# Moving the self products of 24 row blocks into the next stage's first slots, and building one-hots on ScalarE in the last two steps of a graph network

## The chip, the cores and the metric

The kernel runs on one core of a Trainium2 chip. The metric is the device time of one execution in microseconds (us); lower is better. The engines named below are PE (TensorE: matrix products), DVE (VectorE), ACT (ScalarE), POOL (GpSimd, which issues the indirect DMAs that gather rows) and SP (SyncE, which issues the plain DMAs). Everything is float32.

## The reference

There are 10,000 nodes with 512 features and 160,000 edges sorted by destination; every edge has one of four types. Two layers follow each other, each on `h = relu(layernorm(x))` and each with a residual.

```python
# layer 0
h_all = einsum('nd,rdf->nrf', x, rel_W) + rel_b        # one product per node and edge type
agg   = segment_sum(h_all[src, edge_type], dst) / max(deg, 1)
x1    = layer_norm(x + x @ self_W + self_b + agg)      # x here is the layer's h
out   = layer_norm(x1 + gelu(x1 @ W1 + b1) @ W2 + b2)
# layer 1, twice with its own weights
h_neigh = segment_sum(h[src], dst) / max(deg, 1)
h = relu(h @ W_self + h_neigh @ W_neigh + b)
```

## The kernel before

The 10,000 rows are cut into 78 blocks of 128 rows and a last one of 16 rows (block number `full` = 78). The program has three parts, one after the other, because each gathers rows from a DRAM table that the part before must have written completely.

**The relation stage.** It goes over 39 sets of two blocks (and the short block first). For each set it normalizes the rows, transposes them on PE into `hT`, forms the four relation products by a scheme with seven half products instead of eight (`times`, line 717), and writes them to the table `hall_d`. Within it `residual` (lines 648 to 655) forms the self product of each block: four matmuls of `hT` with `wself` (to whose diagonal 1 was added, so that it also carries the residual `x`), then a DVE addition of `bself`; `stored` (lines 663 to 666) writes the sum to `xs_d`. A generator `step` puts the preparation of the edge lists (which rows each block gathers) between these products; its last pieces run in the first half of the last twelve sets. Here the framework's scheduler may reorder instructions.

**The feed-forward stage.** From here on (`aligned`, line 752) the order is as written. One slot per block, the short one first. In a slot the kernel gathers the rows of the next block (`gather`, line 765), builds its one-hot matrices (`hots`, line 782), sums the shared rows with one-hot matmuls (`sums`, line 790) and adds 11 rows per lane with DVE additions (`add`, line 804). A full block takes 11 such gathers (`row`), 5 (`orow`) for `sums`, and now and then one into `tail`; each brings 128 rows of 2 KB. The gathered tiles `rows` come from a ring of 28 buffers. After the additions the slot normalizes its block, and PE runs a piece of the feed-forward products of the group of four blocks before (`queue`, `products`): half of the up products or two down products. The queue is filled when the first block of the next group has gone by, so the first slots have almost nothing in it. The tiles `po`, `h1` and `xr` of the profile belong to this stage; `po` has two PSUM buffers.

**The last two steps.** Each goes over the 79 blocks and gathers from `h1_d` or `h2_d` in the same way. A slot has the self product (`wss`, line 1134), the neighbour product of the block before (`finish`, line 1100), the transposition of the next block, then `begin` for the next block, which gathers and runs `sums`. In all three gathering stages `hots` is one DVE comparison of 128x896 elements per block:

```python
nc.vector.tensor_tensor(hot[:, :n], lane[:, None, :].to_broadcast([P, n, P]),
                        loc[:, b, :n].unsqueeze(2).to_broadcast([P, n, P]),
                        op=OP.is_equal)
```

Of the kernel before, what the change touches and what calls it, by code (L numbers as in the profile page):

```python
# [8 lines left out]
F32 = mybir.dt.float32  # L9
# [3 lines left out]
AF = mybir.ActivationFunctionType  # L13
# [3 lines left out]
P = 128  # L17
# [4 lines left out]
def kernel(  # L22
# [77 lines left out]
    dram = ctx.enter_context(tc.tile_pool(name="dram", bufs=1, space=DRAM))  # L100

    hall_d = dram.tile([N + P, R * D], F32, name="hall_d")
    xs_d = dram.tile([N, D], F32, name="xs_d")
# [484 lines left out]
    with ExitStack() as s:  # L588
# [58 lines left out]

        def residual(rows, r, c, pm):
            xg, _, hg, _ = rows
            h = hg[:r, c, :]  # L650
            nc.vector.tensor_tensor(xg[:r, c, :], xg[:r, c, :], ln2b[:r], op=OP.add)
            for k in range(KC):
                nc.tensor.matmul(pm[:r], rows[3][:, c, k, :r], wself[:, k, :], start=(k == 0),  # L653
                                 stop=(k == KC - 1))
            nc.vector.tensor_tensor(h, pm[:r], bself[:r], op=OP.add)
# [7 lines left out]
        def stored(g, rows):  # L663
            b0, nb, r = g
            nc.sync.dma_start(rows_of(xs_d, g), rows[2][:r, :nb])
            nc.sync.dma_start(rows_of(xr_d, g), rows[0][:r, :nb])
# [7 lines left out]
        if N % P:  # L674
            r = sets[0][2]
            residual(rows, r, 0, psM.tile([P, D], F32, name="pm"))
            for j in sorted(range(R), key=lambda j: (j % RH, j)):
                pm = psM.tile([P, D], F32, name="pm")
                for k in range(KC):
                    nc.tensor.matmul(pm[:r], rows[3][:, 0, k, :r], wrel[j][:, k, :],  # L680
                                     start=(k == 0), stop=(k == KC - 1))
                ha = ap_.tile([P, D], F32, name="u2")
                nc.vector.tensor_tensor(ha[:r], pm[:r], bias(j)[:r], op=OP.add)
                message(full, j, ha, r)
            stored(sets[0], rows)
# [14 lines left out]
        for i, g in enumerate(sets):  # L700
# [7 lines left out]

            def times(pm, a, w, start, stop):
                for k in range(KH):  # L710
                    nc.tensor.matmul(pm, a[:, k, :], w[:, k, :], start=(start and k == 0),
                                     stop=(stop and k == KH - 1))

            def times(a, w):
# [6 lines left out]
            for j in range(RH):  # L721
# [12 lines left out]
                if j == 0 and later:  # L734
                    rows_next = opened(later)
                residual(rows, P, j, psM.tile([P, D], F32, name="pm"))
                if later:
# [14 lines left out]
    def aligned(ctxa):  # L752
# [28 lines left out]

        def hots(b):
            n = OT + NL if b < full else OT_LAST
            hot = gat.tile([P, OT + NL, P], F32, name="hot", bufs=2)
            nc.vector.tensor_tensor(hot[:, :n], lane[:, None, :].to_broadcast([P, n, P]),  # L785
                                    loc[:, b, :n].unsqueeze(2).to_broadcast([P, n, P]),
                                    op=OP.is_equal)
            return hot

        def sums(b, others, hot):  # L790

            r, n = height(b), len(others)
            pa = psA.tile([P, D], F32, name="pa")
            order = list(range(n)) if b == full else list(range(OT, n))[::-1] + list(range(OT))
            for t in order:
                nc.tensor.matmul(pa[:r], hot[:, t, :r], others[t], start=(t == order[0]),  # L796
                                 stop=(t == order[-1]))
            return pa

        def begin(b, hot, table):  # L800
            others, mine = gather(b, table)
            return sums(b, others, hot), mine

# [7 lines left out]
        with ExitStack() as s:  # L811
# [34 lines left out]
            def column(row, name):  # L846
# [3 lines left out]
                return t  # L850

            for b in blocks[:2]:
                load(b)
            ln1w = wide(wp, ln1_w, D, "ln1w")
            lnb2 = wide(wp, ln1_b, D, "lnb2")
# [146 lines left out]
            def products(work, turned):  # L1002
# [10 lines left out]
                if not work:  # L1013
                    yield
                    if turned:
                        turned()
                fed = [g for g in got if g]

            i = 0
            grp = None  # L1020
            for bs in plan:
                for b in bs:
# [5 lines left out]
                    if i + 1 < len(blocks):  # L1028
                        hot = hots(blocks[i + 1])
                    got = second()  # L1030
                    pa, mine = held
# [32 lines left out]
        for step, (h_d, ws, wn, bs) in enumerate(((h1_d, ws1, wn1, bs1), (h2_d, ws2, wn2, bs2))):  # L1064
            with ExitStack() as s:
# [52 lines left out]
                before = None  # L1118
                held = begin(blocks[0], hots(blocks[0]), h_d)
                for i, b in enumerate(blocks):  # L1120
# [4 lines left out]
                    if i + 1 < len(blocks):  # L1125
                        hot = hots(blocks[i + 1])
                    pa, mine = held
# [10 lines left out]
                    if i + 1 < len(blocks):  # L1138
                        turn(blocks[i + 1])
                        held = begin(blocks[i + 1], hot, h_d)  # L1140
                    mT = ip.tile([P, KC, P], F32, name="mTb")
# [4 lines left out]
    def general():  # L1146
# [141 lines left out]
        with ExitStack() as s:  # L1288
# [8 lines left out]
            ln1w = wide(vp, ln1_w, D, "ln1w")  # L1297
            ln1b = wide(vp, ln1_b, D, "ln1b")
            for g in groups:
                b0, nb, r = g  # L1300
# [152 lines left out]
```

## Time and profile before

| | |
|---|---|
| time, median of 3 runs | 6363.47 us (6357.54 to 6369.66) |
| the profiled execution: its own time, its span | 6372.26 us, 6370.5 us |
| mean granted PE clock | 0.935 |
| busy: PE, DVE, ACT, POOL | 5484.2, 3734.8, 1356.8, 3824.4 us |
| relation stage, to the last DVE addition | 0 to 1318 us |
| first gather of the feed-forward stage | 1321.38 us |
| last gather of it | 2975.57 us |
| gathers of the first of the two steps, first and last | 3076.55 and 4708.84 us |
| gathers of the second step, first and last | 4726.08 and 6350.45 us |

The share of busy time of an engine is a mean over stages with different limits. The table of stretches therefore says more than the totals: in the relation stage POOL has little to do, and in the other stages it issues one gather after the other. A row of the groups gives busy time, then the mean duration of one instruction in ns, then the idle time of the engine before these instructions and what ended it. One matmul of 128x512 in float32 is two records.

### The profile page before, as it was taken

What the parts mean: (1) busy time and instruction counts of PE and PEld (TensorE: products, weight loads), DVE (VectorE), ACT (ScalarE), POOL (GpSimd) and SP (SyncE); (2) the same over time, 40 slices, a digit from 0 to 9 for tenths busy, and PEclk for the clock granted to TensorE, in tenths of its full rate; (3) what the DMA queues carried; (4) which work ended last, traced back from release to release, by engine and by line L of the source; (5) the groups of instructions that cost most, each with busy time, mean ns of one, the idle gap of its engine ahead of it and who ended that gap; (6) DMA issues with size and microseconds to landing.
All of it is one profiled execution on the core that took longest, in us unless ns stands there. A gap on an engine that the chain in (4) does not pass through costs nothing.

```text
span 6370.5 us, 50895 instructions
## 1 busy us (share of the span) xinstructions
PE 5484.2 (86%) x13939; PEld 2410.3 (38%) x13939; DVE 3734.8 (59%) x7361; ACT 1356.8 (21%) x2391; POOL 3824.4 (60%) x3927
## 2 busy tenths in 40 slices
PE   9999999969999999999777777777777777777777
PEld 4544444434444444444333333333333333333333
DVE  8768888556777777776344444444444444444444
ACT  1025665013333333333111111111110000000000
POOL 0001110057777777775577777777767777777776
PEclk9999999989999999999888889889889898888998
DMA  4233333267878777886677777777777777777776
GB/s 165 108 116 124 119 119 121 109 211 243 254 246 255 249 253 254 253 256 188 192 232 233 232 231 228 226 233 233 225 237 246 244 241 243 246 246 246 247 237 204
DMA packets 491734, 1360.90 MB, mean 214 GB/s; under 512 B 76606, under 2 KB 76606, under 8 KB 491310
## 3 DMA queue, kind: packets, MB, share of 16 engines
q0 software_dynamic: 308768, 1008.91, 52.1%
q1 hardware_dynamic: 182142, 347.60, 15.3%
q8 instruction: 112, 1.84, 0.1%
q14 instruction: 184, 1.51, 0.1%
q10 hardware_dynamic: 528, 1.05, 0.0%
HBM read 1150.25 MB, written 207.01 MB: 213 GB/s over the span
## 4 chain that ended last, share of the span: by engine, by line
DMA 34%; PE 8%; issue 4%; POOL 4%; DVE 1%; POOLq 0%; ACT 0%; DVEq 0%; SPq 0%; ACTq 0%
DMA rows<-h_d,row 21%; DMA rows<-h_d,orow 12%; PE pa L796 4%; POOL rows L769 4%; PE po L1134 2%; PE po L1100 2%; DMA tail<-h_d,srow 1%; DVE pa L808 1%; PE pT L167 1%; DVE ob L1110 0%; DMA wns<-in_L_gnn_W_neigh_dram 0%; DMA hb<-h_d 0%; POOLq L769 0%; DVE hot L785 0%; POOL tail L769 0%
## 5 line engine op out<-in xcount | busy, mean ns | idle before, releaser
L808 DVE TENSOR_TENSOR pa<-pa,rows 128x512 f32<-128x512 f32 x2574 | 1798.7, 699 | 1999.0 <-DMA rows<-h_d,row 887.4
L796 PE MATMUL pa<-rows,hot 128*128 128x512 f32 (+1 forms) x2358 | 1381.6, 723 | 675.7 <-DMA rows<-h_d,orow 617.6
L769 POOL DMA_INDIRECT rows<-h_d,row x1716 | 1638.1, 955 | 524.1 <-issue 206.2
L796 PEld LDWEIGHTS pa<-rows,hot 128*128 128x128 f32 (+1 forms) x2358 | 488.8, 225 | 1555.5 <-DMA rows<-h_d,orow 1105.5
L769 POOL DMA_INDIRECT rows<-hall_d,row x858 | 868.6, 1012 | 261.4 <-issue 101.8
L769 POOL DMA_INDIRECT rows<-h_d,orow x786 | 795.0, 1012 | 355.1 <-issue 195.1
L769 POOL DMA_INDIRECT rows<-hall_d,orow x393 | 371.9, 946 | 379.9 <-SPq L1449 258.6
L903 PE MATMUL po<-w2s,hid 128*128 128x512 f32 (+1 forms) x1264 | 561.8, 598 | 26.3 <-DVE rest L959 26.2
L796 PE MATMUL pa<-tail,hot 128*128 128x512 f32 x936 | 476.5, 627 | 114.9 <-DMA tail<-h_d,srow 93.8
L1100 PE MATMUL po<-wns,mTb 128*128 128x512 f32 (+1 forms) x1264 | 572.0, 595 | 1.5 <-ACT mTb L168 1.5
L1134 PE MATMUL po<-wss,hTb 128*128 128x512 f32 (+1 forms) x1264 | 573.2, 596 | 0.0
L892 PE MATMUL ph<-x1T,w1s 128*128 128x512 f32 (+2 forms) x1344 | 558.5, 568 | 4.8 <-ACT hid L894 4.8
L1130 ACT ACTIVATE mb<-pa,rdeg 128x512 f32<-128x512 f32 (+1 forms) x158 | 108.5, 687 | 1822.0 <-DVE pa L808 1813.1
L503 POOL DMA_INDIRECT win<-rec_d,at x79 | 75.5, 956 | 578.8 <-PE pe L528 500.1
L903 PEld LDWEIGHTS po<-w2s,hid 128*128 128x128 f32 (+1 forms) x1264 | 236.3, 190 | 321.3 <-issue 279.6
L1100 PEld LDWEIGHTS po<-wns,mTb 128*128 128x128 f32 (+1 forms) x1264 | 239.7, 190 | 307.3 <-issue 305.2
L892 PEld LDWEIGHTS ph<-x1T,w1s 128*128 128x128 f32 x1344 | 249.3, 191 | 281.9 <-issue 271.4
L168 ACT COPY mTb<-pT 128x512 f32<-128x512 f32 (+1 forms) x158 | 91.7, 580 | 1108.6 <-PE pT L167 1108.6
L1134 PEld LDWEIGHTS po<-wss,hTb 128*128 128x128 f32 (+1 forms) x1264 | 229.5, 192 | 232.2 <-issue 232.1
L717 PE MATMUL pm<-wrel,hT 128*128 128x512 f32 x624 | 296.6, 598 | 0.0
L717 PE MATMUL pm<-wrel,s 128*128 128x512 f32 x624 | 293.3, 592 | 0.0
L653 PE MATMUL pm<-wself,hT 128*128 128x512 f32 (+1 forms) x632 | 287.0, 597 | 1.0 <-DVE wself L670 1.0
(272 smaller groups left out, 5249.5 us busy)
## 6 DMA issues: line engine op xcount, KB each, us to landing
hall_d<-p SPq DMA_DIRECT2D x156, 256.0 KB, 2.5
hall_d<-u SPq DMA_DIRECT2D x156, 256.0 KB, 2.4
hb<-h_d SPq DMA_DIRECT2D x38, 1024.0 KB, 7.3
rows<-h_d,row POOLq DMA_INDIRECT x1716, 3.7
xg<-in_x_dram SPq DMA_DIRECT2D x39, 512.0 KB, 3.7
xr_d<-xg SPq DMA_DIRECT2D x39, 512.0 KB, 3.0
xs_d<-hg SPq DMA_DIRECT2D x39, 512.0 KB, 2.8
xs<-xs_d SPq DMA_DIRECT2D x39, 512.0 KB, 7.9
```

Of the source, the lines that this page charges most:

```text
L168: nc.scalar.copy(dest, p[:, :, :r])
L503: nc.gpsimd.indirect_dma_start(out=win[:, c, :], out_offset=None, in_=rec_d, in_offset=bass.IndirectOffsetOnAxis(ap=at[:, c:c + 1], axis=0))
L653: nc.tensor.matmul(pm[:r], rows[3][:, c, k, :r], wself[:, k, :], start=(k == 0), stop=(k == KC - 1))
L717: nc.tensor.matmul(pm, a[:, k, :], w[:, k, :], start=(k == 0), stop=(k == KH - 1))
L769: nc.gpsimd.indirect_dma_start(out=t[:n], out_offset=None, in_=table, in_offset=bass.IndirectOffsetOnAxis(ap=idx, axis=0))
L796: nc.tensor.matmul(pa[:r], hot[:, t, :r], others[t], start=(t == order[0]), stop=(t == order[-1]))
L808: nc.vector.tensor_tensor(pa[:r], pa[:r], t[:r], op=OP.add)
L892: nc.tensor.matmul(ph[:, :n], w1s[:, k, f * P:(f + 1) * P], self.xT[:, k, :n], start=(k == 0), stop=(k == KC - 1))
L903: nc.tensor.matmul(po[:r], self.hid[:, f, c * r:(c + 1) * r], w2s[:, f, :], start=(f == 0), stop=(f == FC - 1))
L1100: nc.tensor.matmul(po[:r], mT[:, k, :r], wns[:, k, :], start=False, stop=(k == KC - 1))
L1130: nc.scalar.activation(m[:r], pa[:r], AF.Copy, scale=rdeg[:r, b:b + 1])
L1134: nc.tensor.matmul(po[:r], hT[:, k, :r], wss[:, k, :], start=(k == 0), stop=False)
```

## The change

The self products of the last 24 blocks (54 to 77, twelve sets) are no longer formed in the relation stage. Their transposed rows `hT` go to a new DRAM tensor `hT_d`, one DMA of 256 KB per block, and `xs_d` of these sets is not written there. The feed-forward stage loads `self_W` and `self_b` again, into buffers of the tiles `xr` and `h1`, fetches 3 of the 24 blocks ahead of its first slot and 4, 4, 3, 3, 3, 4 in the slots 0 to 5 (into tiles of the ring `rows`), forms their products at the end of the slot's piece of PE work and ahead of `begin`, and stores them to `xs_d`, where their own slots load them much later. In the last two steps `hots` is built by ACT: seven activations |loc - lane| of 128x128, and one relu(1 - that) over all 128x896. There `sums` is preceded by three products of the identity matrix with a slice of `wss` into the same PSUM tile, which the first product of `sums` overwrites.

The program's other branch (for edge lists that do not fit, not taken here) gets the products of the 24 blocks too; that part is left out.

```diff
+    LATE_SETS = 12
+    late = list(range(full - 2 * LATE_SETS, full))
+    hT_d = dram.tile([len(late) * P, D], F32, name="hT_d")
...
-        def residual(rows, r, c, pm):
-            xg, _, hg, _ = rows
+        def residual(rows, r, c, b):
+            xg, _, hg, hT = rows
             h = hg[:r, c, :]
             nc.vector.tensor_tensor(xg[:r, c, :], xg[:r, c, :], ln2b[:r], op=OP.add)
+            if b in late:
+                i = late.index(b)
+                nc.sync.dma_start(hT_d[i * P:(i + 1) * P, :], hT[:, c].rearrange("p k n -> p (k n)"))
+                return
+            pm = psM.tile([P, D], F32, name="pm")
             for k in range(KC):
                 nc.tensor.matmul(pm[:r], rows[3][:, c, k, :r], wself[:, k, :], start=(k == 0),
                                  stop=(k == KC - 1))
...
         def stored(g, rows):
             b0, nb, r = g
-            nc.sync.dma_start(rows_of(xs_d, g), rows[2][:r, :nb])
+            if b0 not in late:
+                nc.sync.dma_start(rows_of(xs_d, g), rows[2][:r, :nb])
             nc.sync.dma_start(rows_of(xr_d, g), rows[0][:r, :nb])
...
-        def hots(b):
+        def hots(b, scalar=False):
             n = OT + NL if b < full else OT_LAST
             hot = gat.tile([P, OT + NL, P], F32, name="hot", bufs=2)
+            if scalar:
+                for t in range(n):
+                    nc.scalar.activation(hot[:, t, :], lane, AF.Abs, bias=loc[:, b, t:t + 1],
+                                         scale=-1.0)
+                nc.scalar.activation(hot[:, :n], hot[:, :n], AF.Relu, bias=ones[:, :1], scale=-1.0)
+                return hot
...
+        def keep_busy(p, w, n):
+
+            for _ in range(n):
+                nc.tensor.matmul(p, ident, w, start=True, stop=True)
+
-        def sums(b, others, hot):
+        def sums(b, others, hot, idle=None):
 
             r, n = height(b), len(others)
             pa = psA.tile([P, D], F32, name="pa")
+            if idle:
+                keep_busy(pa, *idle)
...
+            FIRST_LATE, LATE = 3, (4, 4, 3, 3, 3, 4)
+            assert FIRST_LATE + sum(LATE) == len(late)
+            ws = [gp.tile([P, 2, D], F32, name="xr", bufs=3) for _ in range(2)]
+            selfb = gp.tile([P, 2, D], F32, name="h1", bufs=2)[:, 0, :]
+            waiting, arrived = list(late), {}
+
+            def fetch(n):
+
+                for b in waiting[:n]:
+                    i = late.index(b)
+                    t = gat.tile([P, D], F32, name="rows", bufs=RING)
+                    nc.sync.dma_start(t, hT_d[i * P:(i + 1) * P, :])
+                    arrived[b] = t
+                del waiting[:n]
+
+            def residuals():
+
+                for b, t in arrived.items():
+                    po = psO.tile([P, D], F32, name="po")
+                    for k in range(KC):
+                        nc.tensor.matmul(po, t[:, k * P:(k + 1) * P], ws[k // 2][:, k % 2, :],
+                                         start=(k == 0), stop=(k == KC - 1))
+                    nc.vector.tensor_tensor(t, po, selfb, op=OP.add)
+                    nc.sync.dma_start(xs_d[b * P:(b + 1) * P, :], t)
+                arrived.clear()
+
+            for i, w in enumerate(ws):
+                nc.sync.dma_start(w, self_w[i * 2 * P:(i + 1) * 2 * P, :].rearrange(
+                    "(k p) n -> p k n", p=P))
+            nc.sync.dma_start(selfb, bass.AP(tensor=self_b.tensor, offset=self_b.offset,
+                                          ap=[[0, P], [1, D]]))
+            fetch(FIRST_LATE)
             for b in blocks[:2]:
                 load(b)
+            for k in range(KC):
+                at = ws[k // 2][:, k % 2, k * P:(k + 1) * P]
+                nc.vector.tensor_tensor(at, at, ident, op=OP.add)
+            residuals()
             ln1w = wide(wp, ln1_w, D, "ln1w")
             lnb2 = wide(wp, ln1_b, D, "lnb2")
...
+                residuals()
                 fed = [g for g in got if g]
...
                         hot = hots(blocks[i + 1])
+                    if i < len(LATE):
+                        fetch(LATE[i])
                     got = second()
...
-                held = begin(blocks[0], hots(blocks[0]), h_d)
+                held = begin(blocks[0], hots(blocks[0], True), h_d)
...
-                        hot = hots(blocks[i + 1])
+                        hot = hots(blocks[i + 1], True)
...
-                        held = begin(blocks[i + 1], hot, h_d)
+                        held = begin(blocks[i + 1], hot, h_d, (wss[:, 0, :], 3))
```

## The prediction

> **What bounds the kernel now.** I read the table of stretches first, one stretch from each stage (columns: stretch, length, then busy us and instructions of PE, PE's weight loads, DVE, ACT, POOL; then PE clock, DMA share, GB/s).
>
> ```profile
> 960.00:1120.00 160.00, 160.00 (x527) 74.92 (x526) 133.69 (x558) 82.03 (x168) 12.41 (x13) 1.00 0.34 118
> 1280.00:1440.00 160.00, 105.93 (x273) 46.10 (x272) 82.69 (x134) 21.45 (x42) 88.72 (x91) 0.78 0.67 218
> 2080.00:2240.00 160.00, 154.85 (x380) 69.21 (x379) 119.47 (x199) 51.90 (x85) 122.23 (x125) 0.99 0.81 256
> 5120.00:5280.00 160.00, 122.70 (x290) 50.91 (x288) 77.29 (x109) 13.39 (x23) 121.93 (x126) 0.89 0.78 245
> ```
>
> The relation stage (first line) is PE without a gap. In the gathering stages POOL looks only 76% busy, but each gather carries 0.30 us around its 0.945 us, so 125 gathers need 125 x 1.25 = 156 of 160 us. POOL is the bound in both; in the feed-forward stage PE (155 us) is just behind it. Next, POOL's groups in the last two steps and the largest DVE and ACT entries there:
>
> ```profile
> L769 POOL DMA_INDIRECT rows<-h_d,row x1716 | 1638.1, 955 | 524.1 <-issue 206.2 <-DMA rows<-h_d,row 193.1 <-DMA rows<-h_d,orow 58.2
> L769 POOL DMA_INDIRECT rows<-h_d,orow x786 | 795.0, 1012 | 355.1 <-issue 195.1 <-DMA rows<-h_d,row 73.4 <-DMA rows<-h_d,orow 28.9
> L785 DVE TENSOR_TENSOR hot<-lane,loc 128x896 f32<-128x896 f32 x156 | 169.2, 1085 | 34.1 <-PE pa L796 34.1
> L1130 ACT ACTIVATE mb<-pa,rdeg 128x512 f32<-128x512 f32 x156 | 107.2, 687 | 1813.1 <-DVE pa L808 1813.1
> ```
>
> POOL's idle time is 0.30 us times its count: it never waits for a ring buffer. But its means, 955 and 1012 ns, are above 945. The timeline of a slot shows why:
>
> ```profile
> 3250.47 0.95 POOL L769 DMA_INDIRECT rows<-h_d,orow  x1 [0.30 <-DMA rows<-h_d,row]
> 3251.55 1.08 DVE L785 TENSOR_TENSOR hot<-lane,loc 128x896 f32<-128x896 f32 x1
> 3251.72 0.62 ACT L1111 ACTIVATE ob<-ob 128x512 f32<-128x512 f32 x1
> 3251.72 1.73 POOL L769 DMA_INDIRECT rows<-h_d,orow  x1 [0.30 <-DVE ob L1110]
> 3253.75 0.95 POOL L769 DMA_INDIRECT rows<-h_d,orow  x1 [0.30 <-issue]
> ```
>
> A gather that starts under the one-hot comparison ends 0.82 us after it: POOL stands still until DVE is done. Last, the joint of the first two stages: the timeline of its start, then PE's waits from 1318 to 1446.
>
> ```profile
> 1322.83 0.37 SPq L857 DMA_DIRECT2D h<-in_L_gnn_b_dram  x1
> 1331.01 0.69 DVE L859 TENSOR_TENSOR lnb<-lnb,h 128x512 f32<-128x512 f32 x1 [12.90 <-DMA ln1bc<-in_L_gnn_ln_b_dram]
> ...
> PE pa L796 <- DMA rows<-hall_d,orow: 34.1, 4, 11.7
> PE pa L796 <- DVE hot L785: 15.0, 1, 15.0
> PE pa L796 <- DMA tail<-hall_d,srow: 4.7, 1, 4.7
> ```
>
> PE has 54 us of gaps there, which the moved products are to fill.
>
> **Part 1, the relation stage.** In the timeline a self product starts at 1231.35 and PE's next work at 1234.78: 3.43 us. 24 of them are 82 us of a stage that is PE alone. Their DVE additions (L655, 0.69 us) go too. In the first half of the twelve sets the list preparation is there: sets are 32.8 us apart, and DVE is busy for 133.69/160 of that, 27.4 us. After the change PE needs 32.8 - 6.9 = 25.9 us a set and DVE 27.4 - 1.4 = 26.0. They now wait on each other; I take 1 us a set for six sets. The stores swap 12 DMAs of 512 KB for 24 of 256 KB on SP, at 0.37 us of issue each beside a set of 25 us: nothing, as PE waits for no store. **Gain 76 us** (bounds: 65, where DVE loses 3 us a set, and 82).
>
> **Part 2, the first slots.** They take the 24 products again; what counts is how far POOL is held back, as it never idles later.
>
> *Start.* SP now issues first the two halves of `self_W`, the bias and three row blocks, six DMAs of some 0.4 us and 2 MB. A 1 MB weight load took 6.2 us to land in the steps (`wss`), so the products start near 1329. PE is cold (0.84 us a record at 1332, later 0.43): 24 records take about 12.5 us, to 1341. Behind them stand three stores on SP, and behind these all of the parameter loads that DVE's L859 and then `hot` and the first `sums` wait for. The trace shows no SP wait for a store. The Trainium skill's page "DMA: Bandwidth & Descriptors" (section "Anatomy of one DMA — SWDGE (gpsimd) path") says that a semaphore wait happens on the issuing sequencer before dispatch, so later DMAs of that queue wait too. By the rows alone (issues of 0.4 us) the start would slip 3 us plus the PE work, 10 us; by the rule the bias load goes out at 1344, lands 7.9 us later as it does now, and the first `sums` starts at 1353 instead of 1332.4. I take the rule: 20 us.
>
> *Slots.* A slot with n moved products: two run at once on PE, but `po` has two buffers, and the third waits for a DVE addition queued behind this slot's 11 row additions and its normalization. In the trace that normalization runs from 1357.6 to 1362.4, so about 5.5 us after the row additions. Then products 3 and 4 end 9.7 and 13.1 us after the row additions, `sums` takes 6.1 us (14 records of 0.43) and the next 11 additions 8 us: 27 us a slot with four, 24 with three, against POOL's 21. From the start at 1353 the row additions of blocks 0 to 5 end near 1386, 1413, 1437, 1461, 1485, 1512; before they ended at 1357.6, 1375.5, 1395.9, 1416.2, 1437.9, 1459.0. DVE and PE are then 53 us late. POOL may run ahead by the ring of 28, less the tiles of moved rows, which come free only when their store has landed (some 3 us): counted tile by tile, block 6's gathers end near 1508 instead of 1476, 32 us late. From then on POOL runs at its pace of before and can't make up; PE, 20.3 us of work a block (154.85 us for 7.63 blocks) against POOL's 20.96, closes 0.65 us a block and has made up the 21 us between them within the 72 blocks left. The drain of 100 us to 3076 stays. **Loss 33 us** (bounds 12, if only PE's excess of 82 - 54 = 28 us counted and half were absorbed, and 70, if no slot overlapped).
>
> **Part 3, one-hots on ACT.** With no stretched gathers, 2552 gathers save their excess: 1638.1 + 795.0 + 47.3 = 2480.4 us busy, less 2552 x 0.945 = 2411.6, is **69 us gained** (0.44 us a block), all on POOL's path. What ACT does instead: a 128x512 activation from SBUF took 0.80 us (L945) and a 128x1 one 0.295, so 0.42 for 128 elements and 1.19 for 896: 7 x 0.42 + 1.19 = 4.1 us a block, 644 us against DVE's 169. This is covered: ACT waits 1813 us for DVE in front of L1130, 11.6 us a block, and the one-hots stand just ahead of it in ACT's queue. Without that cover it would cost 4.1 us x 156. ACT might stop POOL as DVE does: the gather above ended as DVE's end dictates although ACT worked from SBUF (L1111) beside it, so I take none.
>
> **Part 4, identity products.** 3 x 2 records x 0.43 = 2.6 us a block. PE has 122.70/7.7 = 16.0 us a block at clock 0.89 and POOL now sets 20.4, so they fill idle time; at 18.6 us nothing waits. Do they gain? The rows show PE waiting 4.6 us a block for `orow` and `tail` rows (617.6 + 93.8 us in 156 blocks). The skill's page "TensorE: Matmul & The Clock Gate" (section "What's actually happening") says that one idle window of some 3.4 us brings half rate back, which speaks against them: they run ahead of that wait, not through it. By the rule the clock stays near 0.89; if they kept it at 1.0, PE's own work without them would be 30 x 0.43 + 0.9 = 13.8 us. Both lie under 20.4, so 0 us either way.
>
> **Sum.** -76 + 33 - 69 = -112 us from the profiled execution's 6372.3, to 6260. Its run was 8.8 us above the median of 6363.5; less 112 that is **6252 us**.
>
> **Rivals.** *The first slots eat all of part 1.* For it: PE's gaps (54 us) are smaller than the 82 us moved, the ring and two `po` buffers tie the slots together. Against: POOL may run a block ahead. Loss 76, only part 3 left: 6363 - 69 = 6294. *The slots fill smoothly.* The parameter loads aren't held up and the third product isn't either; loss 10: 6363 - 76 + 10 - 69 = 6228. *The steps give little,* because another transfer or the latency (3.7 us to land) limits the gathers once POOL doesn't stall; against it, the DMA share of 0.78. Half of part 3: 6286. *Slower: PE becomes the bound of the last two steps.* The identity products lengthen each slot; if the clock falls, so does everything. At full clock PE's work is 36 records of 0.43 plus transposes of 0.9: 16.4 us a block. Parts 1 and 2 bring 43 us, so the steps must lose 56 us, 0.36 a block on 20.8: that is PE above 21.2 us, a mean clock under 0.77. At 0.70 a block takes 23.4 us, +2.6 x 156 = 406: about 6720. The row shows 0.89 and more work should not lower it. That ACT's one-hots never reach the path as a gain because POOL isn't stopped by DVE at all is excluded by the timeline above.
>
> **How the numbers follow.** Likeliest course 0.60 (6230 to 6275 from the bounds of the parts); first slots eat it all 0.14; smooth slots 0.12; half of part 3 0.09; slower 0.03; about no change, where part 1 and most of part 3 both come to nothing, 0.02. The range 6212 to 6300 takes in the first three and most of the fourth. A measurement tells 0.2% (13 us) from no change: faster 0.95, same 0.02, slower 0.03.
>
> **What would show it.** Right: L653 has 24 blocks fewer and the relation stage ends near 1242; in the next stage the first `sums` waits behind L912 and comes 31 to 32 us after the stage's first gather (11 before); POOL shows real waits in the first seven slots, some 30 us, and none later; in the steps both groups of gathers have means near 945 ns and each step's gathers span about 1594 us (1632 and 1624 before). Wrong: gather means that stay near 1000 (ACT stops POOL too), POOL waiting for PE or ACT in the steps, gaps in the relation stage's PE, or POOL waits of 70 us in the first slots.

## The result and the profile after

The changed kernel takes 6287.03 us (median of 4 runs, 6282.08 to 6287.47); in the same comparison the kernel before takes 6364.49. The ratio is 0.9877, 95% interval 0.986 to 0.9894: 77 us less. The forecast was 6252, with a range of 6212 to 6300: the direction and the range were right, the gain was overestimated by 35 us. The likeliest course, 6230 to 6275, was missed.

The profiled executions show where. Each program is cut at its gathers (from the timelines of POOL); a stretch runs from the start of one gather to that of another:

| stretch, us | before | after | difference | predicted |
|---|---|---|---|---|
| start to first gather from `hall_d` | 1321.4 | 1240.1 | -81.3 | -76 |
| first to last gather from `hall_d` (feed-forward stage) | 1654.2 | 1717.2 | +63.0 | +33 |
| last of these to the first gather of step 1 | 101.0 | 103.4 | +2.4 | 0 |
| gathers of step 1 | 1632.3 | 1593.5 | -38.8 | -69 for both |
| joint | 17.2 | 15.7 | -1.5 | 0 |
| gathers of step 2 | 1624.4 | 1594.8 | -29.6 | |
| rest | 20.1 | 20.0 | 0 | 0 |

The sum is -85.7, the difference of the two spans (6370.5 and 6284.8). Three of the four sizes were right; the first slots of the feed-forward stage cost almost twice what was set down for them. Of the 35 us, 26 lie in this table: 30 too little for those slots, less 5 that the relation stage gave beyond its forecast. The other 9 lie in the base: the profiled execution of the kernel before took 8 us more than its median (6372.26 and 6364.49), that of the changed kernel did not (6286.86 and 6287.03). In which stage the kernel before had these 8 us, one trace can't tell.

The table of stretches of the changed kernel, one from each stage as before (the second is the start of the feed-forward stage):

```profile
960.00:1120.00 160.00, 159.03 (x525) 74.86 (x524) 143.59 (x578) 82.16 (x167) 10.46 (x11) 1.00 0.44 150
1200.00:1360.00 160.00, 116.05 (x273) 51.47 (x272) 59.20 (x98) 11.26 (x22) 56.17 (x60) 0.83 0.64 211
2400.00:2560.00 160.00, 156.42 (x382) 69.61 (x382) 119.22 (x199) 51.91 (x85) 122.27 (x124) 0.99 0.81 254
5120.00:5280.00 160.00, 139.82 (x342) 60.99 (x341) 69.07 (x101) 35.97 (x80) 121.00 (x129) 0.93 0.80 249
```

In the first line DVE is 143.6 of 160 us and PE 159: the relation stage, with 24 products fewer, is still PE's. The last line has POOL at 121.00 us, almost as before (121.93), but with 129 gathers instead of 126: each is shorter. The groups of the last two steps say the same (the gathers, then the one-hots on ACT):

```profile
L773 POOL DMA_INDIRECT rows<-h_d,row x1716 | 1622.2, 945 | 523.6 <-issue 240.3 <-DMA rows<-h_d,row 156.3 <-DMA rows<-h_d,orow 67.0
L773 POOL DMA_INDIRECT rows<-h_d,orow x786 | 743.1, 945 | 356.0 <-issue 106.0 <-DMA h_d<-h 102.5 <-DMA rows<-h_d,row 53.9
L791 ACT ACTIVATE hot<-lane,loc 128x128 f32<-128x128 f32 x1098 | 337.7, 391 | 0.0
L793 ACT ACTIVATE hot<-hot,ones 128x896 f32<-128x896 f32 (+1 forms) x158 | 163.7, 1036 | 5.1
L1186 ACT ACTIVATE mb<-pa,rdeg 128x512 f32<-128x512 f32 (+1 forms) x158 | 108.5, 687 | 1226.9 <-DVE pa L825 1222.9 <-PE pa L813 4.0
```

Both means are 945 ns (955 and 1012 before). ACT's one-hots cost (337.7 + 163.7)/158 = 3.2 us a block, below the 4.1 estimated, and ACT still waits 1223 us for DVE ahead of L1186. PE waited for these one-hots twice, 3.7 us in all, so they are as good as covered.

The joint of the first two stages is where the missing 30 us are. SP's timeline there (start, duration of the issue):

```profile
1255.44 7.19 SPq L892 DMA_DIRECT2D xs_d<-rows  x3
...
1263.68 0.51 SPq L910 DMA_DIRECT2D h<-in_L_gnn_b_dram  x1
...
1266.35 1.56 SPq L914 DMA_DIRECT2D w1s<-in_L_gnn_W_dram  x1
1267.95 5.17 SPq L915 DMA_DIRECT2D b1s<-in_L_gnn_b_dram  x1
1273.16 5.93 SPq L917 DMA_DIRECT2D w2s<-in_L_gnn_W_dram  x1
1279.14 4.43 SPq L143 DMA_DIRECT2D ln2w<-in_L_gnn_ln_w_dram  x1
1283.61 1.89 SPq L880 DMA_DIRECT2D rows<-hT_d  x4
```

and PE's timeline of the same time:

```profile
1248.15 13.40 PE L889 MATMUL po<-xr,rows 128*128 128x512 f32 x24 [12.21 <-DMA rows<-hT_d]
1273.95 4.65 PE L813 MATMUL pa<-rows,hot 128*16 128x512 f32 x6 [12.40 <-DVE hot L795]
1291.91 15.45 PE L889 MATMUL po<-xr,rows 128*128 128x512 f32 x32 [13.31 <-DMA rows<-hT_d]
```

PE's waits from 1240 to 1450 (us in total, times, longest):

```profile
PE po L889 <- DMA rows<-hT_d: 26.4, 4, 13.3
PE po L889 <- DVE rows L891: 20.3, 5, 7.6
PE pa L813 <- DVE hot L795: 12.4, 1, 12.4
```

Before, PE had 54 us of gaps here, and the moved products were to fill them. It still has 59. A balance closes on that: 82 us of products moved, less 54 of gaps that are gone, plus 59 new ones, is 87; the row additions of block 5 end 221.1 us after the first gather instead of 137.6, which is 83.4 late. So the question for the experiments was which of the new waits are needed. e1 to e8 are single runs.

### The profile page after: what moved, and what is told of

Its sections match the earlier page's. It is cut to its first block, busy times and chain, and to the rows that moved or that the text cites. A ratio compares the mean times of both kernels' runs of the same rounds, so it can differ in the third digit from the quotient of the medians.

```text
span 6284.8 us, 53719 instructions
## 1 busy us (share of the span) xinstructions
PE 5753.7 (92%) x14875; PEld 2566.8 (41%) x14875; DVE 3573.7 (57%) x7207; ACT 1842.8 (29%) x3647; POOL 3756.4 (60%) x3927
## 4 chain that ended last, share of the span: by engine, by line
DMA 29%; PE 14%; issue 4%; POOL 3%; DVE 1%; POOLq 0%; ACT 0%; DVEq 0%; ACTq 0%; SPq 0%
DMA rows<-h_d,row 16%; DMA rows<-h_d,orow 12%; PE pa L813 5%; PE po L1190 4%; POOL rows L773 3%; PE po L1156 3%; PE pa L803 1%; PE pT L170 1%; DVE pa L825 1%; DMA tail<-h_d,srow 0%; DMA hb<-h_d 0%; DVE po L1162 0%; POOLq L773 0%; POOL tail L773 0%; DVE ob L1166 0%
## 5 line engine op out<-in xcount | busy, mean ns | idle before, releaser
L813 PE MATMUL pa<-rows,hot 128*128 128x512 f32 (+1 forms) x2358 | 1242.5, 660 | 373.4 <-DMA rows<-h_d,orow 350.0
L773 POOL DMA_INDIRECT rows<-h_d,orow x786 | 743.1, 945 | 356.0 <-issue 106.0
L813 PEld LDWEIGHTS pa<-rows,hot 128*128 128x128 f32 (+1 forms) x2358 | 449.1, 204 | 1124.5 <-DMA rows<-h_d,orow 723.1
L1190 PE MATMUL po<-wss,hTb 128*128 128x512 f32 (+1 forms) x1264 | 598.5, 618 | 0.0
L773 POOL DMA_INDIRECT rows<-hall_d,orow x393 | 376.6, 958 | 351.2 <-SPq L1520 203.2
L813 PE MATMUL pa<-tail,hot 128*128 128x512 f32 x936 | 447.2, 598 | 24.4 <-DMA tail<-h_d,srow 12.7
L1186 ACT ACTIVATE mb<-pa,rdeg 128x512 f32<-128x512 f32 (+1 forms) x158 | 108.5, 687 | 1226.9 <-DVE pa L825 1222.9
L803 PE MATMUL pa<-wss,ident 128*128 128x512 f32 x936 | 427.5, 593 | 0.0
L791 ACT ACTIVATE hot<-lane,loc 128x128 f32<-128x128 f32 x1098 | 337.7, 391 | 0.0
```

Source lines behind the costliest of these rows:

```text
L773: nc.gpsimd.indirect_dma_start(out=t[:n], out_offset=None, in_=table, in_offset=bass.IndirectOffsetOnAxis(ap=idx, axis=0))
L791: nc.scalar.activation(hot[:, t, :], lane, AF.Abs, bias=loc[:, b, t:t + 1], scale=-1.0)
L803: nc.tensor.matmul(p, ident, w, start=True, stop=True)
L1186: nc.scalar.activation(m[:r], pa[:r], AF.Copy, scale=rdeg[:r, b:b + 1])
L1190: nc.tensor.matmul(po[:r], hT[:, k, :r], wss[:, k, :], start=(k == 0), stop=False)
```

## The experiments

Two readings serve as a ruler, both from the first gather of the feed-forward stage: the start of the 115th gather (it belongs to block 6), and the last gather (the stretch). In the three runs where both are seen undisturbed, the delay of the one is the delay of the other: 61.3 and 63.0 us (changed kernel), 46.0 and 50.1 (e1), 17.3 and 17.2 (e2). What POOL has lost at block 6 it keeps, as the prediction said.

**e1: another order on SP.**

The new order of the issues, in short (not the lines of the kernel):

```
load(blocks[0]), load(blocks[1]); ln1w, lnb2, b2s; ln1wc, ln1bc    # parameters first
ws, selfb, fetch(FIRST_LATE), fetch(LATE[0])                       # slot 0's rows too
w1s, b1s, w2s, ln2w
residuals()                                                        # the three stores last
```

> Only the order of SP's issues at the start of the feed-forward stage changes: the parameter loads that the first normalization and the first product need come first, then the self weights and the row blocks of both the first three products and slot 0, then the large weights, and last the three stores. Theory 1 (SP's order is what the prediction missed: the three stores and the small-element parameter loads stand ahead of what slot 0 needs): the first product of sums comes about 14 us after the stage's first gather instead of 33.9, PE's waits for slot 0's row blocks (13.3 us) and POOL's single wait of 20.6 us shrink, and the stretch from the first to the last gather of the stage falls from 1717 to about 1690. Rival R1 (the moved rows share the ring of gathered rows and free their tiles late): the start recovers, but POOL's waits for stores stay near 49 us and the stretch stays at 1708 or more. Rival R2 (plain excess of PE's work over its gaps): the stretch is 1705 to 1717 as well, and PE shows no gap in the first slots.

Measured: stretch 1704.3, total 6277.08 (one run). PE's wait of 13.3 us for slot 0's rows is gone, and the stretch is 13 us shorter. But the first product of `sums` came 34.2 us after the first gather, not 14:

```profile
1242.81 2.59 SPq L905 DMA_DIRECT2D xr<-in_L_gnn_self_W_dram  x2
...
1246.76 9.83 SPq L880 DMA_DIRECT2D rows<-hT_d  x7
```

```profile
1259.39 13.46 PE L889 MATMUL po<-xr,rows 128*128 128x512 f32 x24 [23.62 <-DMA rows<-hT_d]
1274.10 2.75 PE L813 MATMUL pa<-rows,hot 128*16 128x512 f32 x6 [1.25 <-DVE hot L795]
```

The row blocks, issued behind the parameter loads, now reached PE 11 us later, and `sums` stands behind the first 24 matmul records in PE's program. What stretched the seven fetches to 9.83 us is mostly in SP's waits (1239 to 1340):

```profile
SPq L880 <- DMA xr<-in_L_gnn_self_W_dram: 5.5, 2, 2.9
```

Two of the fetches waited for the landing of the two halves of `self_W`, each of which stands eight places ahead of its fetch in SP's order; the next three loads waited in the same way, each for the load eight places ahead. In this order SP thus also stood before loads that had not landed. So the order of SP counts (theory 1), but this one only exchanged one late piece for another. POOL's waits for stores into `xs_d` fell from 49.1 to 27.9 us, where R1 had them unchanged; R2's lower end (1705) was just missed.

**e2: the moved blocks without their products.** Their rows are still fetched, get the bias and are stored.

```diff
-                    po = psO.tile([P, D], F32, name="po")
-                    for k in range(KC):
-                        nc.tensor.matmul(po, t[:, k * P:(k + 1) * P], ws[k // 2][:, k % 2, :],
-                                         start=(k == 0), stop=(k == KC - 1))
-                    nc.vector.tensor_tensor(t, po, selfb, op=OP.add)
+                    nc.vector.tensor_tensor(t, t, selfb, op=OP.add)
```

> The self products of the 24 moved blocks are left out: their rows are still fetched, get the bias added on VectorE and are stored, so the queue, the ring and the stores are as in the changed kernel, and only TensorE's part is gone. Theory 1 (queue order): most of the loss stays; the three stores still wait for their rows and parameter loads stand behind them, first product of sums 22 to 28 us after the first gather, stretch 1690 to 1700. R1 (ring): POOL still waits for stores, stretch 1690 or more. R2 (PE's excess): the stretch falls to about 1660, within 8 us of the 1654 before the change.

Measured: 1671.4, between the two. Fetching, storing and SP's order alone cost 17 us (`sums` begins 24.5 us after the first gather, 11.0 before the change); the other 46 of the 63 appear only when PE has the products. No single theory of the three was right; the two parts fit a queue whose order is harmful mostly through the PE work that it delays, which e6 tests.

**e3 and e4: the two parts of the steps, one at a time.** e3 leaves the identity products out, e4 makes the one-hots on DVE again.

```diff
e3:
-                        held = begin(blocks[i + 1], hot, h_d, (wss[:, 0, :], 3))
+                        held = begin(blocks[i + 1], hot, h_d)
e4:
-                held = begin(blocks[0], hots(blocks[0], True), h_d)
+                held = begin(blocks[0], hots(blocks[0]), h_d)
...
-                        hot = hots(blocks[i + 1], True)
+                        hot = hots(blocks[i + 1])
```

> The changed kernel without the three identity products a block in the last two steps. Theory (gathers on GpSimd set the steps, the identity products lie in TensorE's idle time): each step's gathers span 1593 to 1595 us as with them, the total is 6287 within 6 us; TensorE's granted clock in the steps falls from 0.92 to about 0.89. Rival (the clock that they hold up is part of the gain): each step is 8 us longer or more, 1602 and up, total 6300 or more.

Measured: steps of 1593.7 and 1593.6 us, total 6287.55 against 6287.03. Its table of stretches, to be held against the last line of the changed kernel's:

```profile
5120.00:5280.00 160.00, 123.63 (x300) 51.87 (x299) 69.73 (x101) 36.18 (x81) 121.01 (x129) 0.90 0.80 249
```

PE does 16 us less in 160 at a clock of 0.90 instead of 0.93, and POOL's 121.01 us with 129 gathers stay. The identity products do nothing for the time, as costed: ACT's one-hots alone give all of the 69 us (3256.7 to 3187.3 for both steps).

> The changed kernel with the one-hots of the last two steps made on VectorE again; the identity products stay. Theory (VectorE's one-hot comparison holds up GpSimd's gathers): the gathers' means go back to 955 and about 1010 ns, each step's gathers span 1625 to 1632 us again, the total is 6287 + 68 = 6355. Rival (the identity products or the clock brought the steps' gain): each step stays at 1594 to 1600, total 6287 to 6299.

Measured: 6337.22 us, so the one-hots on ACT are worth 50 us here, not 68. Step 2 went back as expected (1626.6 us), step 1 only half way (1613.2). The groups:

```profile
L773 POOL DMA_INDIRECT rows<-h_d,row x1716 | 1636.4, 954 | 523.1 <-issue 251.0 <-DMA rows<-h_d,row 149.5 <-DMA rows<-h_d,orow 53.3
L773 POOL DMA_INDIRECT rows<-h_d,orow x786 | 780.9, 994 | 356.4 <-issue 116.7 <-DMA h_d<-h 101.1 <-DMA rows<-h_d,row 54.2
```

The mechanism is confirmed: with the comparison back on DVE, the gathers are longer again. Its size depends on something more, on when in a gather the comparison begins (last section). The identity products alone don't explain the missing 18 us, as step 2, which has them too, went back in full.

**e5 to e7: PSUM buffers, a better order, both.** e5 lets the moved products alternate between `po` and the buffers of `ph`. e6 keeps the self weights and the first three row blocks first, as in the changed kernel, then node rows, `ln1w`, `lnb`, `b2s` and slot 0's rows, then the loads of single elements and large weights, and the three stores last. e7 is both.

```diff
-                    po = psO.tile([P, D], F32, name="po")
+                    po = (psH.tile([P, 4 * P], F32, name="ph") if (q + down) % 2 else
+                          psO.tile([P, D], F32, name="po"))
...
-                residuals()
+                residuals(any(got))
```

> Only the PSUM tiles of the moved products change: they alternate between the two buffers of po and the two of ph, which the first slots hardly use; where a down product holds a po buffer they begin with ph. Theory (third product of a slot waits for VectorE because po has two buffers): TensorE's 20.3 us of waits for L891 go, and the stretch from first to last gather falls from 1717 to about 1700. Rival (queue order at the start decides, the po wait is covered by what comes later): the stretch stays at 1711 to 1717.

> Another order of SP's issues: self weights, bias and the first three row blocks first, as in the changed kernel, then node rows and the row-wide parameters, then slot 0's row blocks, then the loads of single elements (ln1wc, ln1bc, b1s) with the large weights, and the three stores last. Theory 1 (order of the queue): first products at 1248 as in the changed kernel, the first product of sums 13 to 16 us after the first gather, no wait for slot 0's rows above 5 us, stretch about 1695 (e1: 1704, because there the first products came 11 us late behind two loads of single elements). Rival: the stretch stays at e1's 1704 or more, since PE's excess is all that is left.

> e5 and e6 together. If PE's two kinds of wait (for the rows at the start, and for VectorE between two products of a slot) are separate, the gains add: 1717 - 17 - 22 = 1678, total about 6248. If one hides behind the other, the stretch is the smaller of e5's and e6's, about 1695. The floor by PE's excess alone (82 us moved less 54 us of gaps before the change) is 1654 + 28 = 1682, less what the later slots absorb.

These three and all later runs fell on other chips, on which PE's records have standstills of 10 to 20 us that the profile puts down to no instruction ("issue"; more on them under e12), and on which every kernel took about a tenth longer, the one before too. The three took 7014.74, 7022.26 and 6989.86 us, the kernel before 6993.81. The stretches expected (1678 to 1700) cannot be read there: they were 1914, 1918 and 1891. The standstills begin to matter only after the first slots, though: up to 1450 the waits of this name are 1.3, 10.0 and 1.2 us in all, and 8.8 of e6's 10.0 stand ahead of moved products, most of it (8.3) at third products of a slot, where the changed kernel shows its `po` wait. So the ruler is read at the 115th gather (undisturbed values for the changed kernel, e1 and e2):

| kernel | row additions of block 5 end | 115th gather | late against before |
|---|---|---|---|
| before | 137.6 | 149.8 | |
| changed | 221.1 | 211.1 | 61.3 |
| e1, parameters first | 205.2 | 195.8 | 46.0 |
| e2, no products | 155.0 | 167.1 | 17.3 |
| e5, `ph` buffers | 203.2 | 198.2 | 48.4 |
| e6, order | 198.2 | 188.2 | 38.4 |
| e7, both | 183.8 | 179.5 | 29.7 |

The `po` wait is worth 13 us and SP's order 23; together 32, so they are largely separate losses, the first of e7's two cases. In e5 the waits for L891's additions are gone from PE's list. PE's waits of e7 up to 1450 show both all but gone; most of what is left is the landing of rows, 12.0 us for the first and 10.4 in two later slots:

```profile
PE po L890 <- DMA rows<-hT_d: 22.4, 3, 12.0
PE po L890 <- DVE pa L825: 2.3, 1, 2.3
```

SP's own waits (1239 to 1340), first of the changed kernel, then of e7, show the same from the other side: the queue stood behind its stores for 63.9 us, then for 35.2.

```profile
SPq L892 <- DVE rows L891: 63.9, 11, 15.7
```

```profile
SPq L893 <- DVE rows L892: 35.2, 5, 19.7
```

e6's `sums` came 26.5 us after the first gather instead of the 13 to 16 expected: PE has the 24 records of the first three products ahead of it. The 29.7 us that e7 is still late are near the excess of PE's work over its gaps that e7's expectation names (82 - 54 = 28 us), but e7's PE still shows waits, so the agreement may be chance.

**e8 to e11: spread, and e7 again.** e8, e10 and e11 are one kernel: e7 with 3 products ahead, 12 in the first six slots and 9 in every fourth slot up to slot 41, self weights in buffers of their own, and a ring of 24. e9 is e7, timed.

```diff
-            FIRST_LATE, LATE = 3, (4, 4, 3, 3, 3, 4)
+            FIRST_LATE, LATE = 3, [3, 3, 2, 2, 1, 1] + [0, 0, 0, 1] * 9
...
-        RING = 28
+        RING = 24
...
```

> e7, with the moved products spread out: 3 ahead, 12 in the first six slots, the last 9 one in every fourth slot up to slot 41. The self weights and bias get buffers of their own, and the ring of gathered rows falls from 28 to 24 tiles to make room. Theory R2 (what is left is PE's work in the first slots beyond its gaps, and later slots have 0.65 us of idle PE each): stretch 1660 to 1670. Rival (a shorter ring costs GpSimd its lead, in this stage and in the steps): stretch 1680 or more, and each step of the last two stages over 1600 us.

> The kernel of e7 again, on another chip, as on that of e5 to e8 TensorE stood still for some 10 us at a time with no releaser, in all four alike. As for e7: if PE's waits at the start and its waits for VectorE between two products are separate losses, the stretch from first to last gather is about 1678 and the total about 6248; if one hides behind the other, about 1695 and 6265. e1, with another order and the po buffers unchanged, had 1704.

> The kernel of e8 again: e9 with 3 products ahead, 12 in the first six slots and 9 one in every fourth slot up to slot 41, self weights in buffers of their own, ring of 24 tiles. Theory R2 (what is left after the waits is PE's work beyond its gaps, and later slots have 0.65 us of idle PE each): stretch 1660 to 1670, total about 6235. Rival (the shorter ring costs GpSimd its lead): stretch 1680 or more, or steps above 1600 us each.

> The kernel of e8 and e10 once more, since TensorE's standstills of 10 to 20 us, on the chips of e5 to e10, hid what the later slots make of it (in the first slots, before these set in, the row additions of block 5 ended 179 us after the first gather, where the changed kernel had 221). Without standstills, theory R2 (PE's work beyond its gaps is what is left; later slots have idle PE): stretch from first to last gather 1660 to 1670, total about 6235. Rival (the ring of 24 tiles costs GpSimd its lead): stretch 1680 or more, or steps above 1600 us each. With standstills: TensorE sets the stretch, 1850 as in e8.

Measured: all with standstills, so neither the stretch nor the cost of the shorter ring is settled (stretches of 1907 to 1923, steps above 1800, for e9 with its 28 tiles too). e9's 115th gather starts at 179.4, as e7's; that of the spread kernel at 175.8 (e8) and 177.0 (e10), 26 to 27 late; in e11 a standstill of 16.3 us falls into the first slots. Nine products fewer in them gain only 3 us more, but up to the 115th gather PE has 10.1 (e8) and 12.5 us (e10) of standstills where e7 has 1.2. So whether the plain excess of PE's work (R2) was what was left over stays open. e8 took 6996.17 us beside 6993.81 for the kernel before. Against the kernel before on the same chip, the ratios are 0.9956 (0.9932 to 0.9981) for e9, and 0.9886 (0.9844 to 0.9928) and 0.9907 (0.9872 to 0.9943) for the spread kernel.

**e12: the changed kernel on such a chip.**

> The changed kernel itself, to have its time and its first slots where TensorE stands still at times (as in e5 to e11), beside the kernel before on the same chip. If TensorE then bounds the last three stages, the moved products (82 us of PE taken from one stage and given to another) change nothing, one-hots on ScalarE save nothing as GpSimd no longer sets the pace, and the identity products cost up to 2.6 us a block: a ratio of 1.00 to 1.02, the form that the rival 'PE becomes the bound of the last two steps' foresaw. If GpSimd's gathers still count, the ratio stays near 0.988. Row additions of block 5 end 221 us after the first gather in both cases.

Measured: ratio 1.0037 (1.0021 to 1.0053). Here the change makes the kernel slower. PE's two largest waits, from the feed-forward stage's start to the end:

```profile
PE po L1156 <- issue: 708.2, 54, 22.9
PE po L1156 <- ACT mTb L171: 127.9, 37, 17.7
```

The first name is misleading. This is one such standstill, the transposition of `mb`, ACT's copy of it, and the product that reads the copy:

```profile
3531.41 0.60 PE L170 MATMUL pT<-ident,mb 128*128 128x128 f32 x4
3548.30 0.59 ACT L171 COPY mTb<-pT 128x512 f32<-128x512 f32 x1 [23.67 <-remote]
3548.94 3.78 PE L1156 MATMUL po<-wns,mTb 128*128 128x512 f32 x4 [13.50 <-issue]
```

PE goes on 0.05 us after ACT's copy has ended, in all 91 waits of the two rows (836 us). ACT in turn starts its copy a median of 12.9 us after the records' end of the transposes that it reads; in the changed kernel's first trace, over all 158 blocks, this median is 0.04 us. So the loss lies between PE's transposes and ACT's being told of them. Whether PE finishes them later than its records say (the profile models the ends of matmuls) or the signal is late, the trace does not show. PE's 350 us of waits for gathered rows, the sign that POOL sets the pace, are gone, while the gathers' mean is 948 ns. PE and ACT set the pace, as the rival on the slower side had it of PE; but what makes it so are the standstills, not the clock that the rival named. Which part of the change then costs the 0.4% was not tried. The first slots are part of it: the 115th gather starts at 233.0 instead of 211.1, and the stretch is 1988 us where e7, on the same chip, has 1891.

So the spread kernel is faster than the kernel before on two of these chips, and e7's on the one where it was timed. The changed kernel was timed on the third; there it is slower, and e7 and e8, in single runs, took about as long as the kernel before. On a chip without standstills they were not run; from the ruler, e7 would take about 6287 - 32 = 6255 us there and the spread kernel 6287 - 35 = 6252, if its shorter ring costs nothing: estimates both.

## Why the prediction was right, and where it was off

*The bound.* Right: POOL in both gathering stages, PE in the relation stage, with the terms costed at -76 and -69 measured as -81 and -68. One reading of POOL's idle time was rough: the 355.1 us of the `orow` gathers are 119 more than 0.30 us times their count, about the two joints between the stages (101.0 and 17.2). The relation stage lost nothing to DVE; the 1 us a set allowed for it was not needed.

*One-hots on ACT.* Right in sum: the excess over 0.945 us was on POOL's path, all of it. e4 adds that this excess is not a constant: with the one-hots on DVE the steps took 68 us longer than the changed kernel's in the trace before, and 52 in e4's.

*Identity products at nothing.* Right, by e3, for a chip on which POOL sets the pace. The clock did rise with them, from 0.90 to 0.93 in the stretch shown, so the forecast that it stays near 0.89 was a little low; the other half, that either clock leaves PE under POOL's pace, is what kept the time the same.

*The start of the first slots.* The step was sized right: the prediction took the rule that an SP issue that waits for a semaphore holds what stands behind it (against the row reading of 10 us), and foresaw the first `sums` 31 to 32 us after the first gather; it came after 33.9. The Trainium skill's page "DMA: Bandwidth & Descriptors" (section "Anatomy of one DMA — SWDGE (gpsimd) path") states where such a wait takes place, on the issuing sequencer. That the later DMAs of SP then wait too was the prediction's inference, and SP's 63.9 us for L891, with the parameter loads behind, bear it out. The trace before could have settled it: the prediction saw no wait of SP for a store there, but SP's waits over the whole span have this one for the store of the last two steps' results:

```profile
SPq L1113 <- ACT ob L1111: 1014.5, 21, 83.4
```

*The slots.* This is the term that was mis-sized, 33 us set down and 63.0 measured. At 63 it lies nearer to the 76 us of the rival in which the first slots eat all of part 1; that the total still fell into the range owes something to its width. The schedule was "the row additions of blocks 0 to 5 end near 1386, ..., 1512", 64.6 to 190.6 us after the first gather. They ended at 81.4, 110.7, 134.4, 158.9, 190.5 and 221.1. Two terms are missing in it. First, 17 us are lost by the end of block 0, 13.3 of them in PE's wait for slot 0's rows: these were taken to be there, at 0.4 us for each DMA ahead of them, but `w1s`, `b1s`, `w2s` and `ln2w` held SP for 17.1 us, and the fetch went out at 1283.61. The trace before has the same loads at 18.4 us, of which these two are most:

```profile
1326.94 11.61 SPq L864 DMA_DIRECT2D w2s<-in_L_gnn_W_dram  x1
1338.59 4.39 SPq L140 DMA_DIRECT2D ln2w<-in_L_gnn_ln_w_dram  x1
```

Before the change nothing urgent stood behind them. Second, slot 4 took 31.6 us and slot 5 30.6 instead of 24 and 27. In slot 4, the short block's down product holds one of the two `po` buffers, and three moved products go through the other one by one:

```profile
1398.26 3.70 PE L889 MATMUL po<-xr,rows 128*128 128x512 f32 x8
1405.73 6.27 PE L889 MATMUL po<-xr,rows 128*128 128x512 f32 x8 [3.77 <-DVE rows L891]
1412.78 3.70 PE L889 MATMUL po<-xr,rows 128*128 128x512 f32 x8 [0.78 <-DVE rows L891]
```

With both removed (e7) block 5 ends at 183.8, near the schedule though from a `sums` 9 us earlier than it has, and the loss at block 6 is 29.7 against the 33 set down. Why slot 5 was long was not followed further. What followed from the schedule held: POOL absorbed 22 us by its lead (83.4 late at block 5, 61.3 at block 6) and gave nothing back in the 72 blocks after it.

*POOL's waits in the first slots* were foreseen at some 30 us, with 70 as the sign of an error. They were 49 for stores and 13 for `pa`, 62 in all: nearer to the sign of an error, as the loss was.

## What to carry to other kernels

Work moved into another engine's gaps fills them only if its operands are there when the gap is and its result buffers are free: list, for each gap, what the moved instruction waits for, and who else holds its PSUM tile. A queue that issues loads and stores in order should have the stores last, and the loads that hold it longest (read their issue times from the trace) behind everything that the next slot needs. And a gain that rests on one engine's being the bound should be looked at where another engine is slower: here a change of -1.2% became +0.4%.

## What the hardware showed beyond that

*A comparison on DVE holds up the gathers that start under it, but not the other way round.* Setting each comparison's start beside the gathers' in the timelines of both steps (before and e4), a gather that starts 0.04 to 0.9 us after a comparison has begun ends 0.82 us after its end, so it loses 0.9 us at most. One that starts within 0.03 us of the comparison takes its 0.95 us, and the comparison up to 1.16 us instead of 1.08. Where the gather is ahead by 0.05 to 0.9 us, neither is longer: the comparison took 1.09 us at most in all 198 cases, though it lay in the gather's time, and the gather 0.95 in all but four. Two pairs of e4, 70 ns apart in their phase:

```profile
3128.98 0.95 POOL L773 DMA_INDIRECT rows<-h_d,orow  x1 [0.30 <-issue]
3129.00 1.10 DVE L795 TENSOR_TENSOR hot<-lane,loc 128x896 f32<-128x896 f32 x1
...
3213.92 1.08 DVE L795 TENSOR_TENSOR hot<-lane,loc 128x896 f32<-128x896 f32 x1
3213.97 1.85 POOL L773 DMA_INDIRECT rows<-h_d,row  x1 [0.30 <-DMA rows<-h_d,orow]
```

The Trainium skill's page "SBUF — State Buffer" (section "SBUF: two separate sides") describes an exclusive lock between DVE and GpSimd: the shared pair of ports goes to the one that starts first, for the whole instruction. The stretched gathers agree with that; the comparisons that began under a gather and lost nothing do not. How often a comparison catches a gather is a matter of phase: in step 1 46 gathers were stretched before and 29 in e4, by 35.2 and 18.2 us in all (the windows 3100 to 4600, with 72 and 73 comparisons), in step 2 72 and 74, without any change in what DVE does. What sets the phase is open.

The feed-forward stage keeps this loss in both kernels, as its one-hots stay on DVE. In the changed kernel:

```profile
L773 POOL DMA_INDIRECT rows<-hall_d,row x858 | 863.0, 1006 | 298.3 <-issue 117.5 <-DMA rows<-hall_d,row 39.3 <-DMA xs_d<-rows 28.5
```

The stage's 1276 gathers lose 57 us beyond 0.945 us each. By the same sign, an end 0.82 us after that of a DVE instruction, 23 us of it go with the comparison and 34 with four 128x512 operations on two tiles in SBUF (L1037 to L1043). The row additions, whose first input is in PSUM, stretch none. What removing this would gain, with PE close behind POOL, was not tried.

*Four loads hold SP's queue.* `w1s`, `b1s`, `w2s` and `ln2w` took 18.4 us to issue before, 17.1 in the changed kernel, 16.7 in e1 and 20.1 in e7 (5.66 + 1.67 + 7.81 + 4.97), where a small load on a free queue takes 0.4; in e7 nothing that the next slot needs stands behind them. Whether it is the 2 MB of each weight or the single elements of `b1s` was not separated.

*Standstills* of 13 us by PE's records, 54 of them in the two steps of e12, on the three chips of e5 to e12 and in none of the runs before. The cause is open; the relation stage has none: it ends at 1240 us on every chip.
